# A graph layer's row gathers: 24 single rows per step in place of 40, at partitions 96 and up, with 43 fillers

## The chip, the core and the metric

The kernel runs on one core of a Trainium2 chip. The metric is the time of one execution on the device, in microseconds (us). The kernel before took 15322.12 us, the median of 3 runs (15321.51 to 15322.25). The engines are named as the profile names them: PE multiplies matrices, DVE is the vector engine, ACT the scalar engine, POOL is GpSimd, SP issues transfers. A queue of an engine (SPq, ACTq, POOLq, PEq) is the sequencer that issues its work.

## The reference

A graph network's layer over 50,000 nodes with 128 features, and 1,650,000 edges sorted by destination. Each edge carries the source's row, through one of two linear maps by its type; a node's messages are summed, its own map is added, then come relu, a residual and a layer norm:

```python
Xs = X[src]
m_data = Xs @ W_data.T + b_data
m_ctrl = Xs @ W_control.T + b_control
msg = jnp.where((edge_types == 0)[:, None], m_data, m_ctrl)
agg = jax.ops.segment_sum(msg, dst, num_segments=X.shape[0])
out = agg + (X @ W_self.T + b_self)
x = _layernorm(X + relu(out))
```

Sources and destinations are drawn at random; every node has also one edge to itself (a self-loop). With the sort by destination, a node has 33 edges in a row on average.

## The kernel before

**Blocks and steps.** The sorted edges are cut into blocks, and a block into two steps (Q = 2). A step of an ordinary block holds SIZE = R x 128 = 12 x 128 = 1536 edges in 12 columns of 128, then F = 42 fillers, then S = 40 single rows. The first and the last block are plain: only the columns of 128, no fillers, no single rows. The first block has 2 x 1536 edges, an ordinary one BE = 2 x (1536 + 42 + 40) edges, the last one what is left. Ten blocks (GB) are a group, whose lists of sources, destinations and types are loaded together.

**How rows are fetched.** For each column of 128 edges POOL issues one indirect transfer (`gathers`, line 477) that fetches 128 rows of 512 bytes of x by their indices; six of them are a pass, and ten passes have buffers (SLOTS). A gather waits only for PE to have finished with the buffer's last use. Self-loops need no gather, because a block's own nodes are loaded as `xT`; `fill` finds the first F self-loops among a step's 1536 edges and puts the fillers' sources in their places, so that the same 12 gathers fetch them. `left_out_columns`, `left_out_matrix`, `left_out_numbers` and `left_out_rows` add the self-loops so displaced from `xT`. The single rows are fetched by SP and ACT (`single_rows`): each loads the byte offsets of its rows from the tile `at_x` into registers (line 446, here in two loads per block, LOADS = 2, of 20 values on each engine) and then issues one copy of one row of 512 bytes per edge (line 451), 20 per step on either engine. `offsets` makes `at_x` of the list `one_g` (line 435). PE waits once per block until a block's single rows have landed (`rows_fetched`).

**What is done with rows.** DVE writes a matrix `oh` per block that has a one where an edge's destination and type point (`onehot`, line 412) and sums its columns (`counts`, line 420). PE multiplies the gathered rows by it into a step's sums (`products`, line 496), adds the product of the single rows (line 502) and the counts (line 505). The 13th column of `oh` belongs to the single rows: their destinations stand in its first 40 rows, the rest is padding. DVE adds the steps' sums into a window of 112 nodes (`add`, `begin_sums`). `layer` (lines 531 to 535), `moments`, `root` (ACT's square root, line 551), `store` and `store_rows` make the output's rows of the block before.

**Order.** The schedule is written out by hand at the end of `straight`: in each block b four quarters q, in each a pass of six gathers and their products, with the other work in between. Single rows are issued two blocks ahead (AHEAD), the first load and its copies in quarter 0, the second in quarter 1:

```python
            if q < LOADS and not plain(b + AHEAD):
                single_rows(b + AHEAD, q)
```

`fill` runs five blocks ahead (RAHEAD), `onehot`, `counts` and `offsets` two or three. Four fills are done ahead of the first block. Once per group `columns` prepares the next group's lists.

**The way out.** `find_bad` looks whether the edges fit this plan: every destination within its window, windows that overlap, and at least F self-loops among the 1536 edges of each step (`least` below F counts as bad). Where they don't fit, `general` runs after it and computes everything again, with gathers of its own: 400 destination blocks with at least 35 (U) gathers of 128 rows each.

Of the kernel before, what the change touches and what calls it, by code (L numbers as in the profile page):

```python
# [12 lines left out]
F32 = mybir.dt.float32  # L13
BF16 = mybir.dt.bfloat16
U8 = mybir.dt.uint8
I32 = mybir.dt.int32
# [8 lines left out]
D = 128  # L25
# [9 lines left out]
R = 12  # L35
W = 60
Q = 2
PASS = 6
B = 112
C = R * Q  # L40
F = 42
TURNS = (20, 20)
S = sum(TURNS)
LOADS = 2
X = Q * S
R1 = R + 1
C1 = Q * R1
SIZES = [P] * R
SIZE = sum(SIZES)
CE = Q * SIZE  # L50
BE = CE + Q * F + X
NBLK = 2 + (E - CE) // BE
# [4 lines left out]
GB = 10  # L57
GROUPS = -(-NBLK // GB)
GC = GB * C1
AHEAD = 2  # L60
# [21 lines left out]
def plain(b):  # L82

    return b == 0 or b >= NBLK - 1
# [6 lines left out]
def straight(ctx, tc, c, x, x_t, src_t, dst_t, etype_t, src_f, dst_f, etype_f, src_x, dst_first, first_p, out):  # L91
# [17 lines left out]
    eds = ctx.enter_context(tc.tile_pool(name="eds", bufs=2))  # L109
# [3 lines left out]
    stp = ctx.enter_context(tc.tile_pool(name="stp", bufs=3))  # L113
# [13 lines left out]
                   allow_small_or_imprecise_dtypes=True)  # L127
    FILL = Q * F + C1
    small = keep_ps.tile([P, 2 * W + F + 2 * FILL + 2], F32, name="small")
    num_ps, rank_no_ps = small[:, :2 * W], small[:, 2 * W:2 * W + F]  # L130
    lists = [small[:, 2 * W + F + i * FILL:][:, :FILL] for i in range(2)]
    sums_at = [small[:Q * F, 2 * W + F + 2 * FILL + i:][:, :1] for i in range(2)]

# [27 lines left out]
    one_g = {}  # L161

    def load_edges(g):
        t = eds.tile([1, GB * X], I32, name="one_g")
        nc.sync.dma_start(t, src_x[None, g * GB * X:(g + 1) * GB * X])
        one_g[g] = t
        loads[g] = {}
        for name, a in (("s", src_t), ("d", dst_t), ("t", etype_t)):
            t = eds.tile([P, GB, C1], I32, name=name, bufs=1)
            nc.sync.dma_start(t.rearrange("p b c -> p (b c)"), a[:, g * GC:(g + 1) * GC])  # L170
            loads[g][name] = t
        for name, a in (("sf", src_f), ("df", dst_f), ("tf", etype_f)):
            t = eds.tile([GS, F], I32, name=name, bufs=1)
            nc.sync.dma_start(t, a[g * GS:(g + 1) * GS, :])
            loads[g][name] = t


    load_edges(0)
    BL = TBL
    first_i = keep.tile([P, BL, Q], I32, name="first_i")  # L180
# [191 lines left out]
    def chunks_of(b, q):  # L372

        n = RCH if b == NBLK - 1 else C if b < NBLK else 0
        return range(q * R, max(q * R, min((q + 1) * R, n)))

    def column(k):
        return k // R * R1 + k % R
# [13 lines left out]
    bys, pcs, zs, pls, bases, ats, ys = {}, {}, {}, {}, {}, {}, {}  # L392
    ohs, cnts, accs, xTs, pos, hs, mvs, sds, os_ = {}, {}, {}, {}, {}, {}, {}, {}, {}
# [22 lines left out]
    def counts(b):  # L416

        cnt = ohp.tile([P, Q, 2 * W], BF16, name="cnt")
        with nc.allow_low_precision(reason="whole numbers up to R1"):
            nc.vector.tensor_reduce(cnt, ohs[b].rearrange("p (q r) w -> p q w r", r=R1), AX.X, ALU.add)  # L420
        cnts[b] = cnt
# [3 lines left out]
    ROW_SLOTS = AHEAD + 2  # L425
# [4 lines left out]
    def offsets(b):  # L430

        if not plain(b):
            g, i = divmod(b, GB)
            ats[b] = stp.tile([1, X], I32, name="at_x", bufs=AHEAD + 2)
            nc.vector.tensor_scalar(ats[b], one_g[g][:, i * X:(i + 1) * X], float(ROW), None, op0=ALU.mult)

    def single_rows(b, part):

        if part == 0:
            ys[b] = stp.tile([S, Q, D], F32, name="yx", bufs=ROW_SLOTS)  # L440
        both = []
        for j, (eng, dma) in enumerate(((SP, nc.sync), (ACT, nc.scalar))):
            n = Q * TURNS[j]
            k0, k1 = part * n // LOADS, (part + 1) * n // LOADS
            at = Q * sum(TURNS[:j])
            _, rows = nc.values_load_multi_w_load_instructions(ats[b][0:1, at + k0:at + k1], engines=[eng], **RANGE)
            both.append([(dma, fetched[j][b % ROW_SLOTS], *divmod(k0 + k, TURNS[j]), sum(TURNS[:j]), row)
                         for k, row in enumerate(rows)])
        for pair in zip_longest(*both):
            for dma, sem, q, k, at, row in filter(None, pair):  # L450
                copy = dma.dma_start(ys[b][at + k:at + k + 1, q, :].bitcast(U8), x_bytes[:, bass.ds(row, ROW)])
                copy.then_inc(sem, 16)
                tc.no_tile_sem_insts.add(copy.ins.name)
                tc.add_to_no_dep_group(f"single{b}", copy.ins)

    def rows_fetched(b):

        times = len(range(b % ROW_SLOTS or ROW_SLOTS, b + 1, ROW_SLOTS))
        for j in range(2):
            wait = nc.tensor.wait_ge(fetched[j][b % ROW_SLOTS], 16 * Q * TURNS[j] * times)  # L460
        tc.declare_fence(wait.ins, group=f"single{b}")
# [9 lines left out]
    def gathers(b, ks):  # L471
        i = pass_no[0] % SLOTS
        pass_no[0] += 1
        y = gat.tile([P, PASS, D], F32, name="y")
        for k in ks:
            r = REST_ROWS[k] if b == NBLK - 1 else SIZES[k % R]
            copy = nc.gpsimd.indirect_dma_start(  # L477
                out=y[:r, k % PASS, :].bitcast(U8), out_offset=None, in_=x_rows,
                in_offset=bass.IndirectOffsetOnAxis(ap=idxs[b][:r, column(k):column(k) + 1], axis=0))
            copy.then_inc(landed[i], 16)  # L480
            tc.no_tile_sem_insts.add(copy.ins.name)
            tc.add_to_no_dep_group(f"rows{b}_{ks[0]}", copy.ins)
        seen[i] += 16 * len(ks)
        wait = nc.tensor.wait_ge(landed[i], seen[i])  # L484
        tc.declare_fence(wait.ins, group=f"rows{b}_{ks[0]}")
        return y

    def products(b, q, ks):
        y = gathers(b, ks)
        of_step = chunks_of(b, q)  # L490
        if ks[0] == of_step[0]:
            accs[b, q] = ps.tile([P, 3, W], F32, name="acc")
        acc = accs[b, q]
        for k in ks:
            r = REST_ROWS[k] if b == NBLK - 1 else SIZES[k % R]
            nc.tensor.matmul(acc[:, :2, :].rearrange("p t w -> p (t w)"), y[:r, k % PASS, :], ohs[b][:r, column(k), :],  # L496
                             start=k == of_step[0], stop=plain(b) and k == of_step[-1])
        if ks[-1] == of_step[-1]:
            if not plain(b):
                if q == 0:  # L500
                    rows_fetched(b)
                nc.tensor.matmul(acc[:, :2, :].rearrange("p t w -> p (t w)"), ys[b][:, q, :],  # L502
                                 ohs[b][:S, q * R1 + R, :], start=False, stop=True)
            for t in range(2):
                nc.tensor.matmul(acc[:, 2, :], to_row[:, t, :], cnts[b][:, q, t * W:(t + 1) * W],  # L505
                                 start=t == 0, stop=t == 1)
# [87 lines left out]
    for b in range(1, AHEAD + 1):  # L594
        offsets(b)
# [7 lines left out]
    for b in range(1, RAHEAD):  # L603
        fill(b)
        left_out_columns(b)
        left_out_matrix(b)
        if b < AHEAD:
            onehot(b)
            counts(b)
            for part in range(LOADS):  # L610
                single_rows(b, part)
        if b == 1:
            clear_sums()
    for b in range(NBLK + 1):
# [5 lines left out]
        if i == 0 and g + 1 < GROUPS:  # L620
            load_edges(g + 1)
# [9 lines left out]
        for q, (step, ks) in enumerate(passes_of(b)):  # L631
            if ks:
                products(b, step, ks)
# [24 lines left out]
            if q == 3:  # L658
                left_out_matrix(b + RAHEAD)
                offsets(b + AHEAD + 1)  # L660
            if q < LOADS and not plain(b + AHEAD):
                single_rows(b + AHEAD, q)
# [338 lines left out]
```

## Time and profile before

| | |
|---|---|
| median of 3 runs | 15322.12 us |
| the profiled execution: its time | 15323.45 us |
| the profiled execution: its span | 15321.7 us |
| mean granted clock of PE | 0.535 |
| busy: POOL, DVE, PE, ACT | 75%, 71%, 54%, 1% of the span |
| gathers on `idx` and on `s` | 12216 and 24 |
| single-row copies | 20320 on SP's queue, 20320 on ACT's |
| DMA | 939.07 MB, mean 61 GB/s |

The span runs from the first to the last instruction of the profiled execution. A group of instructions is read as: line, engine, operation, written tile <- read tiles, shape, count, then busy us and the mean ns of one, then the idle time of the engine right before them and what ended most of it. "issue" as a releaser means that the engine waited for nothing that the profile shows. In the timeline a row has the start and the length in us, and in brackets the idle time before.

### The profile page before, as it was taken

Reading aid. Unit: us, or ns where it says so; the run is one execution under the profiler, and the core shown is the slowest. Engines: PE = TensorE matmul, PEld = TensorE weight load, DVE = VectorE, ACT = ScalarE, POOL = GpSimd, SP = SyncE. Lnnn points to the kernel's source line nnn. Section 1 sums busy time; section 2 is a strip of 40 time slices with the busy share of each in tenths; the row PEclk is TensorE's granted clock in tenths of the full one; section 3 lists DMA queues with packets and bytes.
Section 4 is the critical chain, followed back from the end, with each engine's and each line's share of the span. In section 5 each row is a group of like instructions: output and inputs, shape, how many; then the busy total and the mean of one; then the engine's idle time right before and its main releaser. Section 6 shows DMA issues by size and latency. Waiting matters only on the chain. (4 is left out here: it accounts for less than half of the span.)

```text
span 15321.7 us, 197234 instructions
## 1 busy us (share of the span) xinstructions
PE 8296.6 (54%) x35844; PEld 7096.5 (46%) x35845; DVE 10904.6 (71%) x13994; ACT 153.6 (1%) x516; POOL 11565.0 (75%) x12250
## 2 busy tenths in 40 slices
PE   3555555555555555555555555555555555555555
PEld 3444444444444444444444444444444444444444
DVE  8777777777777777777777777777777777777775
ACT  0000000000000000000000000000000000000000
POOL 7777777777777777777777777777777777777777
PEclk7555555555555555555555555555555555555555
DMA  2222222222222222222222222222222222222222
GB/s 65 62 61 62 61 62 61 62 62 61 62 61 62 61 62 61 62 61 62 62 60 62 61 62 61 62 62 61 61 62 62 61 62 61 62 61 62 62 61 56
DMA packets 649293, 939.07 MB, mean 61 GB/s; under 512 B 327756, under 2 KB 445487, under 8 KB 648034
## 3 DMA queue, kind: packets, MB, share of 16 engines
q0 software_dynamic: 391680, 802.93, 20.9%
q1 hardware_dynamic: 215276, 112.76, 2.9%
q10 hardware_dynamic: 41078, 10.68, 0.3%
q14 instruction: 968, 7.93, 0.2%
q8 instruction: 291, 4.77, 0.1%
HBM read 895.92 MB, written 29.42 MB: 60 GB/s over the span
## 5 line engine op out<-in xcount | busy, mean ns | idle before, releaser
L477 POOL DMA_INDIRECT y<-in_x,idx x12216 | 11540.9, 945 | 3733.3 <-issue 3552.2
L496 PE MATMUL acc<-oh,y 128*128 128x120 f32 x24480 | 5867.6, 429 | 5768.3 <-PEq L484 5767.8
L496 PEld LDWEIGHTS acc<-oh,y 128*128 128x128 f32 x24480 | 5313.7, 326 | 6190.7 <-PEq L484 6178.3
L420 DVE TENSOR_REDUCE cnt<-oh 128x240 bf16<-128x3120 f32 x510 | 2959.6, 5803 | 0.1
L541 DVE COPY h<-po 112x128 f32<-112x128 f32 x510 | 148.7, 292 | 2499.1 <-PE po L535 2407.5
L412 DVE TENSOR_TENSOR oh<-col,small 128x3120 f32<-128x3120 f32 x510 | 1719.5, 3372 | 0.0
L512 DVE TENSOR_TENSOR sums<-acc,sums 128x180 f32 x1020 | 352.2, 345 | 1393.1 <-PE acc L505 1236.0
L338 DVE TENSOR_REDUCE by<-old 128x84 bf16<-128x1092 f32 x508 | 1078.5, 2123 | 17.6
L502 PE MATMUL acc<-oh,yx 40*128 40x120 f32 x2032 | 777.4, 484 | 0.0
L345 PE MATMUL small<-ones_b,by 128*84 128x1 bf16 x508 | 117.4, 231 | 1191.1 <-DVE by L338 1191.1
L319 DVE TENSOR_TENSOR m<-rk,small 128x1092 f32<-128x1092 f32 x508 | 656.4, 1292 | 17.3
L322 DVE TENSOR_TENSOR new<-m,small 128x1092 f32<-128x1092 f32 x508 | 656.2, 1292 | 17.3
L326 DVE TENSOR_REDUCE v_new<-new 128x26 f32<-128x1092 f32 x508 | 655.8, 1291 | 17.3
L345 PEld LDWEIGHTS <-by 128*84 128x84 bf16 x508 | 74.3, 146 | 1267.3 <-DVE by L338 1267.2
L335 DVE TENSOR_TENSOR old<-m,small 128x1092 f32<-128x1092 f32 x508 | 652.3, 1284 | 0.0
L502 PEld LDWEIGHTS acc<-oh,yx 40*128 40x128 f32 x2032 | 497.5, 304 | 210.0 <-issue 205.3
L535 PE MATMUL po<-wmsgT,sums 128*112 128x128 f32 x2040 | 515.1, 396 | 0.0
L535 PEld LDWEIGHTS po<-wmsgT,sums 128*112 128x112 f32 x2040 | 374.0, 253 | 108.2 <-issue 88.7
L533 PE MATMUL po<-bias,sums 3*112 3x128 f32 x1020 | 350.3, 439 | 0.0
L525 DVE TENSOR_TENSOR sums<-pl,sums 128x336 f32<-128x336 f32 x508 | 257.9, 508 | 85.2 <-DVE sums L512 84.6
L532 PE MATMUL po<-wselfT,xT 128*112 128x128 f32 x1020 | 315.5, 412 | 0.0
L551 ACT ACTIVATE sd<-mv,eps 112x1 f32<-112x1 f32 x510 | 150.4, 295 | 15051.3 <-DVE mv L546 8335.5
(118 smaller groups left out, 4174.2 us busy)
## 6 DMA issues: line engine op xcount, KB each, us to landing
yx<-in_x ACTq DMA_DIRECT2D x20320, 0.5 KB
yx<-in_x SPq DMA_DIRECT2D x20320, 0.5 KB
y<-in_x,idx POOLq DMA_INDIRECT x12216
xT<-in_x_t SPq DMA_DIRECT2D x510, 56.0 KB
out<-o SPq DMA_DIRECT2D x510, 56.0 KB
vf_all<-vd SPq DMA_DIRECT2D x51, 420.0 KB
s<-in_src_t SPq DMA_DIRECT2D x51, 130.0 KB
d<-in_dst_t SPq DMA_DIRECT2D x51, 130.0 KB
```

Of the source, the lines that this page charges most:

```text
L319: nc.vector.tensor_tensor(m, rk_g[g][:, i, :, None].to_broadcast([P, C1, F]), rank_no_ps[:, None, :].to_broadcast([P, C1, F]), op=ALU.is_e ...
L322: nc.vector.tensor_tensor(new.rearrange("p (q r) f -> p q r f", r=R1), m.rearrange("p (q r) f -> p q r f", r=R1), vf.rearrange("p (q f) -> ...
L326: nc.vector.tensor_reduce(v, new, AX.X, ALU.add)
L335: nc.vector.tensor_tensor(old, m, cb[:, :, None].to_broadcast([P, C1, F]), op=ALU.mult)
L338: nc.vector.tensor_reduce(by, old.rearrange("p (q r) f -> p q f r", r=R1), AX.X, ALU.add)
L412: nc.vector.tensor_tensor(oh, col_g[g][:, i, :, None].to_broadcast([P, C1, 2 * W]), num_ps[:, None, :].to_broadcast([P, C1, 2 * W]), op=AL ...
L420: nc.vector.tensor_reduce(cnt, ohs[b].rearrange("p (q r) w -> p q w r", r=R1), AX.X, ALU.add)
L477: copy = nc.gpsimd.indirect_dma_start(out=y[:r, k % PASS, :].bitcast(U8), out_offset=None, in_=x_rows, in_offset=bass.IndirectOffsetOnAxis ...
L496: nc.tensor.matmul(acc[:, :2, :].rearrange("p t w -> p (t w)"), y[:r, k % PASS, :], ohs[b][:r, column(k), :], start=k == of_step[0], stop= ...
L502: nc.tensor.matmul(acc[:, :2, :].rearrange("p t w -> p (t w)"), ys[b][:, q, :], ohs[b][:S, q * R1 + R, :], start=False, stop=True)
L512: nc.vector.tensor_tensor(part, accs.pop((b, q)), part, op=ALU.add)
L535: nc.tensor.matmul(po, a[:, t, :B], c["wmsgT"][:, t * D:(t + 1) * D], start=False, stop=t == 1)
```

## The change

A step has 24 single rows in place of 40, 12 by SP and 12 by ACT, and 43 fillers in place of 42. A block's offsets are read in one load per engine, of 24 values, in quarter 0. The list, the offsets and the rows are placed at partitions 96 and up: each tile is allocated with that many more partitions and used from partition 96 on, and the destinations in the 13th column stand in rows 96 to 119.

```diff
@@ -38,10 +38,11 @@
-F = 42
-TURNS = (20, 20)
+F = 43
+TURNS = (12, 12)
 S = sum(TURNS)
-LOADS = 2
+LOADS = 1
+AT = 96
 X = Q * S
@@ load_edges
-        t = eds.tile([1, GB * X], I32, name="one_g")
+        t = eds.tile([AT + 1, GB * X], I32, name="one_g")[AT:, :]
@@ offsets
-            ats[b] = stp.tile([1, X], I32, name="at_x", bufs=AHEAD + 2)
+            ats[b] = stp.tile([AT + 1, X], I32, name="at_x", bufs=AHEAD + 2)[AT:, :]
@@ single_rows
-            ys[b] = stp.tile([S, Q, D], F32, name="yx", bufs=ROW_SLOTS)
+            ys[b] = stp.tile([AT + S, Q, D], F32, name="yx", bufs=ROW_SLOTS)[AT:, :, :]
@@ products
-                                 ohs[b][:S, q * R1 + R, :], start=False, stop=True)
+                                 ohs[b][AT:AT + S, q * R1 + R, :], start=False, stop=True)
@@ kernel
-        cols[1:NBLK - 1, :, R, :S] = steps[:NBLK - 2, :, SIZE + F:]
+        cols[1:NBLK - 1, :, R, AT:AT + S] = steps[:NBLK - 2, :, SIZE + F:]
```

## The prediction

> **What bounds the kernel now.** I read the page's busy shares first, then its costliest groups.
>
> ```profile
> PE 8296.6 (54%) x35844; PEld 7096.5 (46%) x35845; DVE 10904.6 (71%) x13994; ACT 153.6 (1%) x516; POOL 11565.0 (75%) x12250
> ...
> L477 POOL DMA_INDIRECT y<-in_x,idx x12216 | 11540.9, 945 | 3733.3 <-issue 3552.2
> L496 PE MATMUL acc<-oh,y 128*128 128x120 f32 x24480 | 5867.6, 429 | 5768.3 <-PEq L484 5767.8
> ```
>
> No engine looks full, but one line of POOL carries the span. The row gathers of line 477 have 11540.9 us of busy time and 3733.3 us of idle time in front of them, together 15274.2 of 15321.7 us. The idle time is not waiting: 3552.2 us of it is "issue", which means that nothing the profile shows had to end first. So a gather costs 15274.2 / 12216 = 1.2503 us from start to start. PE waits for the gathers (PEq L484 is its wait for rows that have landed), not they for it. The list of waits, in which the longest wait is the last number, shows how little POOL waits for others:
>
> ```profile
> POOL y L477 <- issue: 3559.2, 11667, 0.3
> ...
> POOL y L477 <- PE acc L496: 3.5, 2, 3.2
> ...
> POOL y L477 <- DVE idx L330: 2.9, 1, 2.9
> ```
>
> Two real waits, both in the first 90 us, then none. The timeline of POOL in the middle of the run (start, length, idle before) shows the beat:
>
> ```profile
> 6999.04 0.94 POOL L477 DMA_INDIRECT y<-in_x,idx  x1 [0.31 <-issue]
> 7000.29 0.94 POOL L477 DMA_INDIRECT y<-in_x,idx  x1 [0.30 <-issue]
> 7001.53 1.11 POOL L477 DMA_INDIRECT y<-in_x,idx  x1 [0.30 <-issue]
> 7002.95 0.95 POOL L477 DMA_INDIRECT y<-in_x,idx  x1 [0.30 <-issue]
> ```
>
> 0.94 + 0.30 us, again and again. A block of 24 gathers lasts 24 x 1.2503 = 30.0 us, and the other engines fit in it with room: DVE 10904.6 / 510 = 21.4 us a block, PE 8296.6 / 510 = 16.3 us. The time is therefore (number of gathers) x (time of one), and the change has to be read for both factors.
>
> **The change part by part: the number of gathers.** A step is 12 gathers of 128 rows, F fillers that take places of self-loops among those rows, and S single rows that SP and ACT copy. Fillers and single rows ride along without a gather. Before, a step covers 1536 + 42 + 40 = 1618 edges and a block of two steps 3236. After, 1536 + 43 + 24 = 1603 and 3206. Of the 1,650,000 edges, 3072 are in block 0. Before, (1,650,000 - 3072) // 3236 = 508 full blocks and a rest of 3040 edges, in 24 gathers: 24 + 508 x 24 + 24 = 12240, the page's 12216 and the last block's 24. After, // 3206 = 513 full blocks and a rest of 2250, in 12 + 6 = 18 gathers (17 full ones and one of 74 rows): 24 + 513 x 24 + 18 = 12354. That is 114 more: 114 x 1.2503 = **+142.5 us**. With the 1.245 to 1.25 us between undisturbed starts it is 141.9 to 142.5.
>
> The Trainium skill says otherwise ("DMA: Bandwidth & Descriptors", section "Issuing engines are not separate DMA queues"): starting DMAs from several engines saves only the sequencer's time to start them, usually small beside the DMA itself. By that rule moving 16 rows a step from SP and ACT back to POOL would be about free, and the time would stay at 15322; here the time to start a gather is the whole span, so the row decides against it.
>
> **One more group.** 515 blocks are 52 groups of ten instead of 51, so `columns` runs once more. Its DVE work delays two gathers: the one at 7001.53 above took 1.11 instead of 0.94 us, and one at 6997.69 took 1.04. That is **+0.27 us** once.
>
> **Fillers 42 to 43.** In `fill`, four DVE operations go from 26x42 to 26x43 elements. The slope from two rows of the page, 3372 ns for 3120 elements (L412) and 1292 ns for 1092 (L319), is 1.026 ns an element: 26 more are 0.027 us, four times 0.107. The strided reduction L338 grows by the slope between 5803 ns (L420) and 2123 ns: 1.815 ns, 0.047 us. Together +0.15 us a block, DVE 21.4 to 21.55 of 30.0: hidden under the gathers; uncovered it would be 513 x 0.15 = 79 us. Only the start is not hidden. POOL's two waits hang on DVE: gather 24 on the first `idx`, gather 60 on PE freeing the first row buffer, which stands in PE's queue behind the columns of four fills. Four times 0.15 is 0.6; ten more blocks in `base`, `begin` and `shift` (1.2 us for 1020 elements, now 1040) add some 0.1: **+0.7 us**, taken between 0 and 1.5.
>
> **Single rows.** From the timelines of SP and ACT and the list of what reads `at_x`:
>
> ```profile
> 7014.69 14.42 SPq L451 DMA_DIRECT2D yx<-in_x  x40
> ```
> ```profile
> 7014.83 6.78 ACTq L451 DMA_DIRECT2D yx<-in_x  x20
> 7021.72 0.29 ACT L551 ACTIVATE sd<-mv,eps 112x1 f32<-112x1 f32 x1 [36.07 <-issue]
> ```
> ```profile
> L446 ACTq TENSOR_LOAD <-at_x x1016: 1411/1437/1689, 16.8 to 15202.4; - x170
> L446 SPq TENSOR_LOAD <-at_x x1016: 1197/1378/1676, 26.8 to 15191.8; - x170
> ```
>
> A copy costs its queue 14.42 / 40 = 0.36 us and a load of 20 values 1.38 (SP) or 1.44 us (ACT). One load of 24 values isn't in the trace: between 1.4 us if it is the instruction that costs, and 24 / 20 x 1.44 = 1.7 if it is the values; I take 1.7. SP falls from 40 x 0.36 + 2 x 1.4 = 17.2 us a block to 24 x 0.36 + 1.7 = 10.3, ACT likewise. Neither is late now, so that is worth nothing. What moves is the order: all 24 copies of ACT now stand ahead of `root` (L551) where 20 did. Root, at 7021.72 right behind the 20 copies, comes 4 x 0.34 + 0.3 = 1.7 us later. DVE's `rstd` waits for it, and starts at 7027.64, behind the 5.8 us of `counts`: 6 us of cover, cost 0. Without cover it would be 1.7 us on a DVE with 8.5 us of room. On SP `store_rows` and the next `window` stand behind the copies, and get earlier.
>
> **Partitions 96 and up.** Nothing in the trace sits there alone. For PE, the two products with 40 rows took 0.48 us each, and those with 3 rows (L533) 0.44; I take 0.48 for 24 rows at 96, up to double (a further 1 us a block) as the bound, against 14 us of idle PE. For the load and the offsets' multiplication (0.19 us) I take no difference. For the gathers beside the copies the bounds come from gathers: from the shortest beat that the trace has (the least distance between two starts, 1.244 us) to two delayed gathers in every block as beside `columns`. That is 12354 x (1.2503 - 1.244) = -78 us to 513 x 0.27 = +139 us. I take 0, because the beat of ordinary blocks is nearest.
>
> **Sum.** 142.5 + 0.3 + 0.7 = +143.5. The profiled span is 15321.7, that execution's time 15323.45 (1.75 around the span), and the median of the runs 15322.12, so 1.33 under the profiled one. Span 15465.2, time **15465.6**, 0.94% more. About 0.2%, 31 us, is what a measurement of this kernel tells from no change.
>
> **Rivals.** *The gathers get shorter, and the time isn't longer.* The rows leave partitions 0 to 39, and 40% of the small copies disappear; if those copies delay POOL now, the beat falls. To break even it must fall by 143.5 / 12354 = 11.6 ns, to 1.2387. Against it: the gathers at the start, before the first copy was started at 18.35 us, and those at the end, after the last copy at 15210, have the same beat:
>
> ```profile
> 5.89 0.94 POOL L477 DMA_INDIRECT y<-in_x,idx  x1 [0.30 <-issue]
> 7.13 0.94 POOL L477 DMA_INDIRECT y<-in_x,idx  x1 [0.30 <-issue]
> 8.38 0.94 POOL L477 DMA_INDIRECT y<-in_x,idx  x1 [0.30 <-issue]
> ```
>
> Even the shortest beat of the trace everywhere gives 15465.6 - 78 = 15388, still slower. Break-even or better needs a beat that no row shows: 0.03, half of it under 15291. The Trainium skill's pages would let one hope: "DMA: Bandwidth & Descriptors" (section "Latency and other measured facts") guesses that the rings of descriptors that POOL writes lie on partitions 0 to 31 and make their ports busy, and "SBUF — State Buffer" (section "Door 1: The DMA port swizzle") puts partitions 64 and up on other ports; neither gives a figure for a gather.
>
> *The gathers get longer.* If `fill` at an odd width, or the rows' new place, delays two gathers in each block as `columns` does, 15465.6 + 139 = 15605. For it: such delays exist (1.11 us). Against: `fill` runs in every block now and leaves no such mark. 0.04.
>
> *The straight path is refused.* `find_bad` compares the fewest self-loops of a step with F; below it, `general` runs as well, with at least 400 x 35 = 14000 gathers of 1.25 us, +17500, some 33000 us. I counted the reference's edges: the fewest among a step's 1536 gathered rows are 43 in both layouts, and the test is "fewer than 43": it holds without any room. 0.01.
>
> **How the numbers follow.** The sum has 0.92. Its own width is small: runs agree within 1 us, the start is open by 1, the beat by a few ns in 114 gathers. A tenth of either bound on the beat (8 us below, 14 above) is let in for the new place: 15458 to 15479. Slower 0.92 + 0.04 + 0.01 = 0.97, within 0.2% 0.015, faster 0.015.
>
> **What would show it.** The changed profile should have 12336 gathers on `idx` and 18 on `s`, at 945 ns busy and 305 ns idle each; 24 x 513 = 12312 single copies on each of the two queues, and 513 loads of `at_x` on each; `fill`'s rows at 1.32 and 2.17 us; DVE still at 71% and PE at 54%. A beat other than 1.250, a third wait of POOL, or a PE that waits for single rows would make the forecast wrong.

## The result, and the profile after

The changed kernel takes 15468.28 us, the median of 4 runs (15466.40 to 15471.34), against 15321.83 us before (4 runs): 1.0096 times as long, with a 95% interval of 1.0078 to 1.0113. That is 0.96% slower, where 0.94% was forecast, and 2.7 us above the forecast 15465.6. The profiled execution has a span of 15466.8 us, 1.6 above the forecast 15465.2.

The page after, the same groups as those shown of before, and the lines of its list of waits that answer to POOL's:

```profile
PE 8387.4 (54%) x36190; PEld 7171.1 (46%) x36191; DVE 11141.1 (72%) x14143; ACT 155.0 (1%) x521; POOL 11673.6 (75%) x12364
...
L478 POOL DMA_INDIRECT y<-in_x,idx x12336 | 11654.8, 945 | 3769.4 <-issue 3597.8
L497 PE MATMUL acc<-oh,y 128*128 128x120 f32 x24708 | 5932.4, 430 | 5621.5 <-PEq L485 5621.5
```
```profile
POOL y L478 <- issue: 3603.3, 11816, 0.3
...
POOL y L478 <- PE acc L497: 4.8, 4, 3.9
POOL y L478 <- DVE idx L331: 3.3, 2, 3.0
```

Line 478 is what line 477 was. It has 120 gathers more and everything else about it is the same: 945 ns of work, (11654.8 + 3769.4) / 12336 = 1.2503 us from start to start, the value of before to the fourth digit. With 18 instead of 24 gathers on `s` that is 12354, 114 more. PE still waits for POOL, DVE has gone from 71% to 72%, and POOL has the same two real waits at the start, each a little longer. So the extra time lies in the number of gathers, and no engine became a new bound.

What the change does to the queues of SP and ACT is visible too, and worth nothing. A block's turn on ACT, and the loads, of the changed kernel:

```profile
7015.77 7.86 ACTq L452 DMA_DIRECT2D yx<-in_x  x24
7024.02 0.30 ACT L552 ACTIVATE sd<-mv,eps 112x1 f32<-112x1 f32 x1 [36.78 <-issue]
```
```profile
L447 ACTq TENSOR_LOAD <-at_x x513: 1647/1668/1785, 16.8 to 15333.3; - x171
L447 SPq TENSOR_LOAD <-at_x x513: 1579/1585/1679, 26.8 to 15333.7; - x171
```

24 copies take 7.9 us on ACT; before, 40 took 14.4 us on SP, with the block's second load among them. The square root follows behind all 24 of them, and DVE's `rstd` starts at 7027.77, still behind `counts`.

The one thing in the difference that the forecast did not have stands at the end, in the chain of waits. First before, then after (start, length, what):

```profile
15305.30 2.44 DMA y<-in_x,s
```
```profile
15447.81 3.89 DMA y<-in_x,s
```

The last gather fetches 96 rows before and 74 after, and 74 rows land later. From the last gather's start to the end of the span it is 15321.7 - 15305.30 = 16.4 us before and 15466.8 - 15447.81 = 19.0 after. From the first gather to the last it is 142.5 us more.

### The profile page after: what moved, and what is told of

Its sections match the earlier page's. It is cut to its first block, busy times and chain, and to the rows that moved or that the text cites. A ratio compares the mean times of both kernels' runs of the same rounds, so it can differ in the third digit from the quotient of the medians.

```text
span 15466.8 us, 165309 instructions
## 1 busy us (share of the span) xinstructions
PE 8387.4 (54%) x36190; PEld 7171.1 (46%) x36191; DVE 11141.1 (72%) x14143; ACT 155.0 (1%) x521; POOL 11673.6 (75%) x12364
## 5 line engine op out<-in xcount | busy, mean ns | idle before, releaser
L478 POOL DMA_INDIRECT y<-in_x,idx x12336 | 11654.8, 945 | 3769.4 <-issue 3597.8
L339 DVE TENSOR_REDUCE by<-old 128x86 bf16<-128x1118 f32 x513 | 1112.0, 2168 | 17.7
L346 PE MATMUL small<-ones_b,by 128*86 128x1 bf16 x513 | 118.7, 231 | 1335.9 <-DVE by L339 1321.9
L503 PE MATMUL acc<-oh,yx 24*128 24x120 f32 x2052 | 785.6, 483 | 0.0
L346 PEld LDWEIGHTS <-by 128*86 128x86 bf16 x513 | 75.1, 146 | 1414.1 <-DVE by L339 1414.1
L323 DVE TENSOR_TENSOR new<-m,small 128x1118 f32<-128x1118 f32 x513 | 677.3, 1320 | 17.5
L320 DVE TENSOR_TENSOR m<-rk,small 128x1118 f32<-128x1118 f32 x513 | 677.3, 1320 | 17.4
L327 DVE TENSOR_REDUCE v_new<-new 128x26 f32<-128x1118 f32 x513 | 676.1, 1318 | 17.5
L336 DVE TENSOR_TENSOR old<-m,small 128x1118 f32<-128x1118 f32 x513 | 673.4, 1313 | 0.0
L503 PEld LDWEIGHTS acc<-oh,yx 24*128 24x128 f32 x2052 | 502.0, 303 | 213.5 <-issue 209.9
```

The source lines that it names most:

```text
L320: nc.vector.tensor_tensor(m, rk_g[g][:, i, :, None].to_broadcast([P, C1, F]), rank_no_ps[:, None, :].to_broadcast([P, C1, F]), op=ALU.is_e ...
L323: nc.vector.tensor_tensor(new.rearrange("p (q r) f -> p q r f", r=R1), m.rearrange("p (q r) f -> p q r f", r=R1), vf.rearrange("p (q f) -> ...
L327: nc.vector.tensor_reduce(v, new, AX.X, ALU.add)
L336: nc.vector.tensor_tensor(old, m, cb[:, :, None].to_broadcast([P, C1, F]), op=ALU.mult)
L339: nc.vector.tensor_reduce(by, old.rearrange("p (q r) f -> p q f r", r=R1), AX.X, ALU.add)
L478: copy = nc.gpsimd.indirect_dma_start(out=y[:r, k % PASS, :].bitcast(U8), out_offset=None, in_=x_rows, in_offset=bass.IndirectOffsetOnAxis ...
```

## The experiments

Theory: the time is the number of gathers times 1.2503 us, whatever runs beside them, as long as SP's and ACT's own work of a block fits in the block's 30 us. Rivals: the place of the single rows matters, the width of `fill` matters, or the copies beside a gather delay it. All runs but `rows_30_36` stand against a kernel before of 15321 to 15323 us on the same chip.

**The place alone, in both directions.** `place_0` takes the changed kernel back to partition 0:

```diff
-AT = 96
+AT = 0
```

> The change with the list, the offsets and the rows back at partition 0 (24 rows, 12 and 12, one load, 43 fillers stay). 12354 gathers as with the change. Theory (time = gathers x 1.2503 us, whatever runs beside them): 15466 to 15471, beat 1.2503. Rival (the place at 96 shortens or lengthens a gather): away from 15468 by more than 30 us, with a beat away from 1.250 by more than 2.5 ns.

Measured: 15467.22 us, ratio 1.0094 (1.0077 to 1.0111). `place_64` gives the kernel before the changed kernel's placement code with AT = 64 and its 40 rows:

```diff
+AT = 64
...
-            ys[b] = stp.tile([S, Q, D], F32, name="yx", bufs=ROW_SLOTS)
+            ys[b] = stp.tile([AT + S, Q, D], F32, name="yx", bufs=ROW_SLOTS)[AT:, :, :]
...
```

> The kernel before, with the list, the offsets and its 40 rows at partitions 64 and up (64 to 103) and nothing else changed. 12240 gathers. Theory: 15320 to 15325, beat 1.2503. Rival (rows at partitions 0 to 39 disturb what POOL does there): faster by up to 78 us, 15244 to 15290, with a beat towards 1.244.

Measured: 15322.29 us, ratio 1.0000 (0.9990 to 1.0009). POOL's gathers in the list of groups by line, at 0 and at 64:

```profile
L478 POOL DMA_INDIRECT y<-in_x,idx x12336 | 11654.1, 945 | 3768.6 <-issue 3579.3 <-DVE h L543 72.1 <-DVE mv L547 34.0
```
```profile
L478 POOL DMA_INDIRECT y<-in_x,idx x12216 | 11540.7, 945 | 3733.5 <-issue 3555.7 <-DVE h L543 74.5 <-DVE mv L547 34.2
```

945 ns and 1.2502 and 1.2503 us from start to start. The place of the list, the offsets and the rows costs and gives nothing.

**43 fillers alone.**

```diff
-F = 42
+F = 43
```

> The kernel before with 43 fillers instead of 42 and nothing else. A block covers 3238 edges, the rest is 2024 edges in 16 gathers: 12232 gathers, 8 fewer. Theory: -8 x 1.25 = -10.0, and +0.7 at the start from the longer fills: 15311 to 15315; DVE 0.15 us busier a block. Rival (the odd width of fill delays POOL): +79 to +139 us on it, 15390 to 15450.

Measured: 15311.72 us (10 runs, 15310.43 to 15314.28), ratio 0.9993 (0.9983 to 1.0003), and 11.3 under the 15322.98 of before on that chip. Eight gathers fewer are 10.0. The gathers themselves are as before, so the odd width delays nothing:

```profile
L477 POOL DMA_INDIRECT y<-in_x,idx x12216 | 11541.2, 945 | 3732.1 <-issue 3554.0 <-DVE h L542 77.3 <-DVE mv L546 33.3
```

**Twice the copies.** Each single row is also copied into a tile that nobody reads.

```diff
...
+                for to in (yd[b], ys[b]):
-                copy = dma.dma_start(ys[b][at + k:at + k + 1, q, :].bitcast(U8), x_bytes[:, bass.ds(row, ROW)])
+                    copy = dma.dma_start(to[at + k:at + k + 1, q, :].bitcast(U8), x_bytes[:, bass.ds(row, ROW)])
...
-            wait = nc.tensor.wait_ge(fetched[j][b % ROW_SLOTS], 16 * Q * TURNS[j] * times)
+            wait = nc.tensor.wait_ge(fetched[j][b % ROW_SLOTS], 2 * 16 * Q * TURNS[j] * times)
```

> The change with every single row copied twice, the second time into a tile that nobody reads: 48 copies a block on SP's queue and 48 on ACT's, more than before the change. 12354 gathers. Theory: the copies hide, beat 1.2503, 15466 to 15472; ACT's square root stands behind 48 copies (48 x 0.33 + 1.7 = 17.5 us after the offsets), so DVE should now wait for it some 2 to 5 us a block, inside its 8.5 us of room. Rival (copies beside a gather delay it): a beat longer than 1.2503 by 2.5 ns or more, 15500 and up.

Measured: 15472.15 us (15470.40 to 15474.58). Its group of gathers, and a line of its list of waits:

```profile
L480 POOL DMA_INDIRECT y<-in_x,idx x12336 | 11656.3, 945 | 3771.0 <-issue 3571.0 <-PE acc L499 53.3 <-DVE h L545 46.5
```
```profile
DVE rstd L560 <- ACT sd L554: 782.6, 276, 4.3
```

24,624 copies more, and the gathers are at 1.2506 us. DVE now waits for the square root, 782.6 us in 276 waits of at most 4.3 us, where the changed kernel waits 0.4 us in all. That is 1.5 us a block, less than the 2 to 5 that were expected. The cover that the prediction named for `root` is real, has an end, and what leaks out of it goes into DVE's idle time. Of the 53.3 us in front of gathers that are put down to PE, the usual 0.30 us for each of 164 gathers are 49; the time is 4 us longer than the changed kernel's. Twice the copies cost 0.25 ns a gather, not the 2.5 of the rival.

**More single rows instead of fewer.** If only the count of gathers matters, the change went the wrong way along its own knob. `rows_48`:

```diff
-TURNS = (20, 20)
+TURNS = (24, 24)
```

> The kernel before with 24 single rows on each queue per step, 48 instead of 40 (42 fillers, partition 0, two loads of 24 values). A block covers 3252 edges: 506 full blocks and a rest of 1416 edges in 12 gathers, 12180 gathers, 60 fewer. Theory: 15322 - 60 x 1.2503 = 15247, within 4. Rival (the copies' queues have no room left): a beat above 1.2503, a time of 15322 or more.

Measured: 15248.44 us, ratio 0.9952 (0.9936 to 0.9969), 73.3 us under the before of that chip; 75.0 by the count. The beat is (11494.7 + 3719.3) / 12168 = 1.2503 us:

```profile
L477 POOL DMA_INDIRECT y<-in_x,idx x12168 | 11494.7, 945 | 3719.3 <-issue 3544.4
```

`rows_64`:

```diff
-F = 42
-TURNS = (20, 20)
+F = 43
+TURNS = (32, 32)
-LOADS = 2
+LOADS = 4
```

> The kernel before with 32 single rows on each queue per step (64 a step), 43 fillers and four loads of 16 values a block. 503 full blocks... 501 of them ordinary; by the edges: 12054 gathers, 186 fewer. Theory: 15322 - 186 x 1.2503 + 0.7 = 15090, within 6, as long as a queue's own work fits in a block: 64 x 0.36 + 4 x 1.1 + 3 x 0.4 = 28.6 us of 30.0. Rival (the queues are full before that): PE waits for single rows, POOL for buffers, 15150 and up.

Measured: 15105.49 us (15104.93 to 15106.80), ratio 0.9859 (0.9842 to 0.9875): 1.4% faster than the kernel before, and 2.3% under the changed one. The count asked for 15090; the 15 us more were not foreseen. Some 5 of them are the end behind the last gather's start, 21.5 us for 16.4 (perhaps because the last block holds only six gathers); another 9 are a beat of (11389.5 + 3683.5) / 12048 = 1.2511 us:

```profile
L477 POOL DMA_INDIRECT y<-in_x,idx x12048 | 11389.5, 945 | 3683.5 <-issue 3527.1
```

I took SP's queue, late in the blocks where a group's lists are loaded, for the cause, and tried fewer, longer loads, `rows_64_by_32` (LOADS = 2, 32 values each, else as `rows_64`):

> 64 rows a step with two loads of 32 values on each queue instead of four of 16. By 1.38 us for 20 values and 1.59 for 24 a load of 32 takes 2.0, so a queue's work falls from 64 x 0.32 + 4 x 1.23 + 1.3 = 26.8 us to 25.9. Theory (the 15 us over 15090 in the first run came from SP's queue being late where a group's lists are loaded): 15090 to 15100. Rival: no difference to 15105.

Measured: 15108.52 us, 3 us more and not 10 less. A load of 32 values took 2.12 us and one of 16 had taken 1.23, so SP's sum fell by 0.7 us a block of the forecast 0.9, and the time did not follow. The waits of POOL speak against a late queue more directly: those for PE's products (PE acc L496) add up to 22.8 us in 64 waits in the first run and 47.3 us in 144 in the second, and but for one of 3.6 us at the start each is the usual 0.30. What is longer is the gathers themselves, 945.3 and 945.8 ns in the mean where the kernel before has 944.7. Why they are longer stays open.

**Where the queues are full.** `rows_72`:

```diff
-F = 42
-TURNS = (20, 20)
+F = 43
+TURNS = (36, 36)
-LOADS = 2
+LOADS = 4
```

> As with 64 rows a step, but 36 on each queue (72 a step, four loads of 18 values): 11996 gathers, 244 fewer. A queue's work is 72 x 0.36 + 4 x 1.25 + 3 x 0.4 = 32.1 us a block, over the 30.0 of the gathers. Theory: the bound moves to SP's queue, 500 x 32.1 = 16050, between 15200 and 16100; SP is never idle, and POOL waits for PE. If the gathers still set the time: 15322 - 244 x 1.2503 = 15017.

Measured: 18524.46 us, ratio 1.2098 (1.2078 to 1.2118): the direction as forecast, 2400 us past the range. The gathers' group, PE's wait for single rows (PEq L460), SP's timeline, and the loads:

```profile
L477 POOL DMA_INDIRECT y<-in_x,idx x11976 | 11312.2, 945 | 7088.5 <-PE acc L496 3678.7
```
```profile
PE acc L502 <- PEq L460: 5539.1, 445, 25.9
```
```profile
7035.59 33.29 SPq L451 DMA_DIRECT2D yx<-in_x  x72
7069.13 0.34 SPq L563 DMA_DIRECT2D out<-o  x1
7069.71 0.36 SPq L406 DMA_DIRECT2D xT<-in_x_t  x1
7071.82 6.18 SPq L451 DMA_DIRECT2D yx<-in_x  x18
```
```profile
L446 SPq TENSOR_LOAD <-at_x x1992: 1394/2839/4166, 27.1 to 18466.8; - x200
```

A gather is still 945 ns of work, but POOL now waits for PE, PE for single rows, and SP hardly stops (its waits add up to some 390 us of 18500): 7071.82 - 7035.59 = 36.2 us a block. The copies are not slower; the loads are. On both queues they alternate, 1.6 to 1.7 and 3.9 us on SP, 1.8 and 4.1 on ACT, and the slow ones are the second and the fourth of a block, which start 72 and 216 bytes into the queue's part of the list, that is 8 past a multiple of 16. Two tests: the same 72 rows in loads of 24, which all start on multiples of 16 bytes, and the kernel before with its list moved by two values.

```diff
-LOADS = 4
+LOADS = 3
```

> 72 rows a step as before, with three loads of 24 values on each queue instead of four of 18. In the run with four loads every second load of a queue, the ones that start 8 bytes past a multiple of 16 bytes, took 3.93 us and the others 1.65. Theory (the start of the list's piece makes a load slow, and these loads made the queue the bound): loads of 1.6 to 1.7 us, a queue's work 72 x 0.32 + 3 x 1.6 + 1.3 = 29.3 us a block, just under the gathers' 30.0: 15017 if no group's transfers come in between, 15120 with them. Rival (72 copies a block on a queue are too many by themselves): 17000 and more.

```diff
-            ats[b] = stp.tile([1, X], I32, name="at_x", bufs=AHEAD + 2)
+            ats[b] = stp.tile([1, X + 4], I32, name="at_x", bufs=AHEAD + 2)[:, 2:X + 2]
```

> The kernel before with the offsets' tile shifted by two values, so that every load of 20 values starts 8 bytes past a multiple of 16. Theory (start): loads of 3.5 to 4.5 us instead of 1.4, SP's queue 17.2 + 5 = 22 us a block, still hidden: 15320 to 15326. Rival (the odd number of values made them slow, not the start): loads of 1.4 us.

`load_at_8` took 15328.09 us (15327.23 to 15330.33), 5.6 over its before and 2 over the range, and its loads are:

```profile
L446 ACTq TENSOR_LOAD <-at_x x1016: 4422/4477/4720, 16.0 to 15209.3; - x170
L446 SPq TENSOR_LOAD <-at_x x1016: 4071/4266/4557, 26.1 to 15202.5; - x170
```

4.27 and 4.48 us where 20 values took 1.38 and 1.44: the start alone triples a load. (The gathers are a little longer here too, 945.5 instead of 944.7 ns in the mean, which makes 9 us and covers the 5.6; why is not shown.) `rows_72_by_24` took 16013.73 us, ratio 1.0451 (1.0433 to 1.0468), with all loads at 1.68 to 1.77 us: that took 2511 us off, so the loads were most of the excess, but the 15120 that I expected at most was wrong. SP's block and its waits:

```profile
7033.60 27.18 SPq L451 DMA_DIRECT2D yx<-in_x  x72
7061.05 0.34 SPq L563 DMA_DIRECT2D out<-o  x1
7061.63 0.36 SPq L406 DMA_DIRECT2D xT<-in_x_t  x1
7063.77 11.24 SPq L451 DMA_DIRECT2D yx<-in_x  x28
```
```profile
SPq L174 <- DMA out<-o: 534.6, 48, 13.4
```

This block takes 30.2 us, a hair over 30.0, and the median of all is 30.5 from one block's first load to the next one's. So nothing is left over to catch up with what a group adds: its seven further list transfers, and a wait of 534.6 / 48 = 11 us in front of one of them that I had not put into the sum. The 50 blocks with these transfers take 45 us each, 14.6 us more than the median. Together 498 x 0.5 + 50 x 14.6 = some 980 us, and the run is 997 us over the 15017 of the count.

**Unequal turns.** `rows_30_36` gives SP 30 and ACT 36 rows a step (TURNS = (30, 36), LOADS = 3, 43 fillers).

> 66 rows a step, 30 on SP's queue and 36 on ACT's, three loads each (20 and 24 values), 43 fillers: 12040 gathers, 200 fewer than before. SP, which alone has the groups' lists to load, has 60 x 0.32 + 3 x 1.4 + 1.3 = 24.7 us a block; ACT's block took 29.95 us in the run with 72 rows, of 30.0. Theory: 15322 - 200 x 1.2503 = 15072, and 15 more at most, so under the 15105 of 64 rows. Rival (ACT's queue, with no room left, becomes the bound): 15110 and more, POOL waiting for PE.

Measured: 22668.06 us. It says nothing about 15072, because it ran on another chip, on which the kernel before took 19249.89 us (7 runs, 19203.03 to 19318.98). There 66 rows a step are 1.1786 times as long as before (1.1749 to 1.1823), and POOL waits for PE (6175.9 us of the idle time in front of gathers). There the beat of the gathers that wait for nothing is the same 1.25 us. The copies differ:

```profile
7036.93 53.16 ACTq L451 DMA_DIRECT2D yx<-in_x  x72
7090.19 0.29 ACT L551 ACTIVATE sd<-mv,eps 112x1 f32<-112x1 f32 x1 [54.78 <-issue]
```

53 us for what took 28 in `rows_72_by_24`. Copy by copy, stretches at the usual 0.32 us alternate with stretches in which each instruction of the queue takes about 0.7 us. Why the sequencers run so there stays open, and so does how the changed kernel would do on that chip.

## Why the prediction was right

**The count and the beat.** Both factors came out as worked: 12336 and 18 gathers, 1.2503 us each; 142.5 us more from the first gather's start to the last one's, against 142.5 + 0.3 + 0.7 in the sum. That the first number is met to a tenth is partly luck: `place_0`, with the same gathers, has 140.8. The two waits at the start grew from 2.9 to 3.0 and from 3.2 to 3.9 us, +0.8 for the forecast 0.7.

**The covered work.** `fill`'s operations take 1.32 and 2.17 us as forecast, and DVE 11141.1 / 515 = 21.6 us a block (forecast 21.55), still inside 30. A load of 24 values takes 1.59 and 1.67 us: the price grows with the values and is not one per instruction, and 1.7 was the right end. The 0.36 us for a copy was misread: the 14.42 us of SP's 40 copies hold the block's second load, and without it a copy is (14.42 - 1.38) / 40 = 0.33 us, as on ACT. So the queues' turns, 17.2 us before and 10.3 after in the prediction, are some 1.4 and 0.8 us too long. Both are covered, so nothing followed for the time. The products of 24 rows at 96 take 483 ns, as those of 40 rows at 0.

**The rivals.** The gathers got neither shorter nor longer: `place_0`, `place_64`, `fill_43` and `copies_twice` each take one of their causes alone and leave 945 ns. The prediction's own argument from the start of the trace rests on three gathers. The six behind them, also before the first copy, took 1.02 to 1.64 us, so that stretch has no clean beat to compare with, and `copies_twice` is the test that counts. The rule of the Trainium skill that using several issuing engines usually saves little ("DMA: Bandwidth & Descriptors", section "Issuing engines are not separate DMA queues") would have had 24, 40, 48 and 64 rows a step alike; measured are 15468, 15322, 15248 and 15105. The straight path was kept: the profile has no gathers beyond the 12354.

**The size that was off.** The end was left as it was in the sum: no term for a last gather of 74 rows in place of 96. It is 2.6 us longer, 1.45 of them in the landing of these rows. Less the 1.0 us that the gathers stayed under the sum, this makes the 1.6 us of the span. `last_128` fetches 128 rows there (the 54 more are padding), and makes the same edit in `products`:

```diff
-            r = REST_ROWS[k] if b == NBLK - 1 else SIZES[k % R]
+            r = P if b == NBLK - 1 else SIZES[k % R]
```

> The change with the last gather made over 128 rows instead of 74 (the 54 more are padding that no destination takes). The last gather of the change took 1.35 us and its rows landed 3.89 us later in the chain, where those of 96 rows before took 0.92 and 2.44. Theory (74 rows are spread badly over the DMA engines): 0.94 and about 2.4 again, the tail after the last gather's start 1.7 us shorter, 15466.5. Rival (the tail's length is chance): no difference.

Measured: 15467.59 us against 15468.28, too near to tell apart; but the gather itself, in the timeline, and its landing, in the chain of waits, come back:

```profile
15449.12 0.94 POOL L478 DMA_INDIRECT y<-in_x,s  x1 [0.30 <-issue]
```
```profile
15449.12 2.94 DMA y<-in_x,s
```

0.94 us instead of 1.35, landing after 2.94 instead of 3.89 (3.74 and 3.53 in `place_0` and `copies_twice`, which also end with 74 rows). So the row count is the cause for the gather's length, and for most of the later landing. The whole end, from the last gather's start, is 17.3 us here; with 74 rows it is 19.0, 18.0 and 17.7 in the three runs, so the rest of the 2.6 us differs by as much between runs.

## What to carry to other kernels

When one engine issues at a constant beat and waits for nobody, count its instructions before and after: that number times the beat is the change, and everything that lies beside it is worth nothing until it no longer fits. A knob that shifts work from the full engine to queues with room should be turned until those queues' own sum nears the beat, here, on the chips where the kernel before takes 15322 us and of the numbers measured there, 64 rows a step (15105 us) and not 24 (15468 us) or 72 (16014 us at best). That sum needs every instruction of the queue with its measured time, the loads of registers and the rare transfers of a group with their waits too, and some room: on the chip where `rows_30_36` shows a queue's instructions slow in stretches, while unhindered gathers keep their beat, the kernel before took 19250 us as well. That it was slow there for the same reason is likely but not shown.

## What the runs showed of the hardware

- A register load's time depends on where its values start: 20 values took 1.38 us on SP from a place at a multiple of 16 bytes in the list, and 4.27 us from one 8 bytes further. At multiples of 16 it grows with the values: 1.23 (16), 1.38 (20), 1.59 (24), 2.12 us (32).
- The last gather's length depends on its row count, and not in proportion: 944 ns for 128 rows, 923 for 96, 1355 for 74, 1002 for 100 (`rows_72`) and 887 for 8 (`rows_48`). The Trainium skill has a rule that fits ("DMA: Bandwidth & Descriptors", section "Why a DMA increments its semaphore by 16 and not by 1"): a transfer uses the largest number of DMA engines up to 16 that divides the slowest dimension of both its sides. That is 16 for 128 and 96 rows and 2 for 74. The packets in the trace agree: the last gather's rows come in 16 packets of 3072 bytes (six rows each) before, in 16 of 4096 bytes in `last_128`, and in eight of 4096 and two of 2560 bytes after. The ten run as two chains side by side, each with 4 x 4096 + 2560 = 18944 bytes, which is 37 rows of 512.
- Rows at partitions 0 to 23, 0 to 39, 64 to 103 and 96 to 119 left a gather at 945 ns, so the relief of ports that the two pages named in the prediction let one hope for does not show.
